# Router logits of a two-layer attention and expert kernel: each tile of 128 tokens in its own 32 columns of the array, one transpose for four tiles

## The chip, the core and the metric

The kernel runs on one core of a Trainium2 chip. A core has four engines that compute: TensorE (PE in the profile, with its weight loads as PEld), VectorE (DVE), ScalarE (ACT) and GpSimd (POOL); SyncE (SP) issues most transfers. Matmul results land in PSUM[...]; VectorE and ScalarE copy them on to SBUF. The metric is the time of one execution on the device, in microseconds; lower is better. Everything here is fp32.

## What is computed

The program is a stack of two layers over x of shape (4, 512, 256). Each layer is an attention over a context of 1024 rows, and then a mixture of experts with two experts for each token. The change concerns only the logits of the two routers:

```python
def _L0_ffn_ref(x, gate_w, expert_bias, w1, w2):
    logits = jnp.einsum('btd,ed->bte', x, gate_w) + expert_bias     # 8 experts and 4 "zero" ones
    topk_logits, topk_idx = jax.lax.top_k(logits, TOP_K)
    topk_w = jax.nn.softmax(topk_logits, axis=-1)
...
def _L1_ffn_ref(x, Wg, alpha, ln_w, ln_b, fc1_w, fc1_b, fc2_w, fc2_b):
    logits = xf @ Wg                                                # 8 experts
    top_vals, top_idx = jax.lax.top_k(logits, TOP_K)
    gate_score = jax.nn.softmax(top_vals, axis=-1)
...
x = x + _L0_xattn_ref(_layernorm(x, axis=-1), ctx_1024, ...)
x = x + _L0_ffn_ref(_layernorm(x, axis=-1), ...)
x = x + _L1_xattn_ref(_layernorm(x, axis=-1), ctx_1024, ...)
x = x + _L1_ffn_ref(_layernorm(x, axis=-1), ...)
```

## The kernel before

The work goes by batches of 512 tokens (four tiles of 128). `layer0_attention` runs the first attention batch by batch; `layer0_experts` computes keys and values for the second attention beside the last routing steps (`mha_kvs`), and then the expert tiles (`moe`, with `tile_turn`, `tile_up`, `tile_down`); `layer1_attention` runs 32 units of the second attention (a batch, a tile of tokens, a pair of heads each), with the routing of layer 1 and some expert tiles worked in; `layer1_experts` is the last stage, the rest of the second layer's expert tiles.

TensorE's instructions stand in the order in which the Python code issues them (`manual_schedule`); SyncE's too, in the expert stages. The other engines are ordered by a scheduler. What a change moves on those engines is read from the built program.

Routing is a generator, `route_steps(L, b)`, one for each layer and batch, whose steps are taken between pieces of other work. Its steps, each up to a `yield`:

1. `route_norm`: layer norm of x (L807 to L845).
2. Eight transposes of the normed rows into `xT`, [128 features, 2 halves, 512 tokens] (L237, copied out at L243, L245 and L247).
3. The logits, transposed (L858 to L865): two accumulating matmuls, with the router's weights (128 x 12 or 128 x 8) as the loaded operand and the 512 tokens as the moving one. The result, 12 or 8 partitions by 512 tokens, is copied to SBUF at L863 (layer 0, with the bias added for each partition) or at L865 (layer 1).
4. Four transposes, one for each tile of tokens, back to [128 tokens, tile, expert] (L869), a copy to `rt_lg` (L871), and `top2` (L745 to L777).
5. The counts of tokens for each expert and their running sums: two matmuls into `pos` (L886, L887), then each token's row in the experts' buffer, and the scatters to it on GpSimd's queue (L920).

When the last batch of a layer has been routed, `tile_table` makes the table of expert tiles. The first rows of the expert stage (L1182) are loaded after all scatters of the layer; their transposes (L1091) wait for them on TensorE.

PSUM pools of two buffers each: scores `ps_s`, transposes `ps_t`, and the rest `ps_m` (`mm_ps`), from which the logits, their transposes and the sums take a buffer, as do the queries (L586), keys (L485) and values (L499) around them.

Other places that are named below: `sim_finish` with the attended context (`hq`, L334), its product with the encoder (`ehT`, L338), the batch's summary (`hc`, L353 and L355; `hcc`, L382), the mixed weights (`weff`, L388) and the sums that use them (`hcq`, L370, added to x at L396); `sim_scores` (L304); `mha_scores` (L602, L611, L615), `mha_turn` (L625, L628, L630), and `mha_values` (L650), which computes two heads at once, each in its own 64 columns of the array:

```python
for j in range(NJ):
    for r in range(2):
        nc.tensor.matmul(
            op[r * HD : r * HD + HD, :], st["v"][:, j, bass.ts(2 * n + r, HD)], aT[:, r, bass.ts(j, P)],
            start=(j == 0), stop=(j == NJ - 1),
        )
```

The router's weights and bias are loaded once, on SyncE's queue behind the first loads of x and the context (L185 to L187).

Of the kernel before, what the change touches and what calls it, by code (L numbers as in the profile page):

```python
# [8 lines left out]
F32 = mybir.dt.float32  # L9
# [4 lines left out]
ALU = mybir.AluOpType  # L14
# [3 lines left out]
P = 128  # L18
NB = 4
S = 512  # L20
NT = S // P
# [3 lines left out]
NC = D // P  # L25
NH = 4
HD = 64
EX = 8
ET0 = 12
FF0 = 512  # L30
FF1 = 1024
# [2 lines left out]
REGION = NB * S  # L34
ROW = D + 2
TILES = NB * S * 2 // P + EX - 1
RING = 3
W1ROW = NC * FF1 + 2 * NC + FF1 // P
ATT_SCALE = 0.125
# [23 lines left out]
def two_layers(ctx: ExitStack, tc: tile.TileContext, io, out):  # L63
    nc = tc.nc

    const = ctx.enter_context(tc.tile_pool(name="const", bufs=1))
# [14 lines left out]
    def t4(shape, name, dt=F32):  # L81
        return k4.tile(shape, dt, tag="k4", name=name)
# [4 lines left out]
    def tsmall(shape, tag, dt=F32):  # L87
        return sm.tile(shape, dt, tag=tag, name=tag, bufs=2 if tag[:3] in ("rt_", "tp_", "tt_") else None)
# [7 lines left out]
    def mm_ps(name):  # L96
        return ps_m.tile([P, 512], F32, tag="m", name=name)


    ident = const.tile([P, P], F32, tag="ident", name="ident")  # L100
# [23 lines left out]
    nc.gpsimd.tensor_copy(base, base_i)  # L124
    tile_i = const.tile([P, TILES], I32, tag="tile_i", name="tile_i")
    nc.gpsimd.iota(tile_i, [[1, TILES]], base=0, channel_multiplier=0)
    tile_f = const.tile([P, TILES], F32, tag="tile_f", name="tile_f")
    nc.gpsimd.tensor_copy(tile_f, tile_i)
# [14 lines left out]
    def small(name, shape, src, queue=nc.sync):  # L143
        t = const.tile(shape, F32, tag=name, name=name)
        queue.dma_start(out=t, in_=src)
        return t
# [35 lines left out]
    for b in range(2, NB):  # L182
        load_x(b)
        last_load = load_ctxT(b)
    gate_w = small("gate_w", [P, NC, ET0], io["gate_wT"].rearrange("(c p) e -> p c e", p=P))  # L185
    gate_b = small("gate_b", [ET0, 1], io["expert_bias"])
    wg = small("wg", [P, NC, EX], io["Wg"].rearrange("(c p) e -> p c e", p=P))  # L187
    alpha = small("alpha", [P, EX], io["alpha"].partition_broadcast(P))
    fc2b = small("fc2b", [EX, D], io["fc2_b"])
    wq = small("wq", [P, NC, D], io["Wq"].rearrange("(c p) n -> p c n", p=P))  # L190
# [4 lines left out]
    for e in range(EX):  # L195
        i = nc.gpsimd.dma_start(
            out=rows[e * REGION : (e + 1) * REGION, :].rearrange("(p k) r -> p k r", p=P),
            in_=zeros.unsqueeze(1).to_broadcast([P, REGION // P, ROW]),
# [5 lines left out]
        out=ys[:, :].rearrange("(p k) d -> p k d", p=P),  # L204
        in_=zeros[:, 0:D].unsqueeze(1).to_broadcast([P, 2 * NB * S // P, D]),
# [34 lines left out]
    def to_sbuf(dst, src, name, only=None):  # L240
        for c, pt in transposed(src, name):
            if only is not None:
                L1.turned = only(dst[:, c, :], pt)  # L243
            elif c % 2 == 0:
# [155 lines left out]
    def layer0_attention():  # L400
# [31 lines left out]
        for b in range(NB):  # L432
# [32 lines left out]
            if more:  # L465
                turns(b + 1, 3)
            route = route_steps(L0, b)
            next(route)
        return route
# [198 lines left out]
    def layer1_attention(sts):  # L668
# [10 lines left out]
        for i in range(len(units) + 4):  # L679
# [44 lines left out]
            if k == 0 and 0 <= b < NB:  # L724
                routes[b] = route_steps(L1, b)
                next(routes[b])
        scatter_pending(2, L1.normed)
        for n in PIECES:
            for _ in range(n):
                next(tiles, None)  # L730
            for route in routes.values():
                next(route, None)
            if len(L1.run) < NB:
                scatter_pending(2, L1.turned)
            if len(L1.run) == NB and L1.table is None:
                L1.table = tile_table(L1)
# [40 lines left out]
        return w  # L777

    class Layer:
        def __init__(self, n, ne, nf, w, bias):  # L780
            self.n, self.ne, self.nf, self.w, self.bias = n, ne, nf, w, bias
            self.run = []
            self.state = {}
            self.done = None
            self.table = None

            self.first = (0, 0, 0) if n == 0 else (0, 0, 1)
            self.spread = []
            self.held = const.tile([P, RING], F32, tag=f"held{n}", name=f"held{n}")
            for s, e in enumerate(self.first):  # L790
                nc.gpsimd.memset(self.held[:, s : s + 1], float(e))

    L0 = Layer(0, ET0, FF0 // P, gate_w, gate_b)
    L1 = Layer(1, EX, FF1 // P, wg, None)
    scatters, row_loads, y_stores = [], [], []
    pending = []

# [49 lines left out]
    def route_steps(L, b):  # L847

        ne = L.ne
# [5 lines left out]
        only = nc.vector.tensor_copy if L.n == 1 and b + 1 == NB else None  # L855
        xT = to_sbuf(t4([P, NC, S], f"xn{L.n}rT_{b}"), L.state[b]["xn"], f"xn{L.n}rTp_{b}", only)
        yield
        lt_ps = mm_ps(f"lgT{L.n}_{b}")[0:ne, :]  # L858
        for c in range(NC):
            nc.tensor.matmul(lt_ps, L.w[:, c, :], xT[:, c, :], start=(c == 0), stop=(c == NC - 1))  # L860
        lt = t4([ET0, S], f"lgTs{L.n}_{b}")[0:ne, :]
        if L.bias is not None:
            nc.vector.tensor_scalar(lt, lt_ps, L.bias, None, ALU.add)  # L863
        else:
            nc.vector.tensor_copy(lt, lt_ps)  # L865
        yield
        lgp = mm_ps(f"lg{L.n}_{b}")[:, 0 : NT * ne].rearrange("p (t e) -> p t e", e=ne)
        for t in range(NT):
            nc.tensor.transpose(lgp[:, t, :], lt[:, bass.ts(t, P)], ident[0:ne, 0:ne])  # L869
        lg = tsmall([P, NT, ne], "rt_lg")  # L870
        nc.vector.tensor_copy(lg, lgp)  # L871
        st = L.state.pop(b)
        buf, xn = st["buf"], st["xn"]
        shape = [P, 2, NT, ne]
# [1 line left out]
        w = top2(lg, ne, pick)  # L876
# [16 lines left out]
        at = tsmall([P, NT, ne], "rt_atp")  # L893
# [81 lines left out]
    def tile_table(L):  # L975

        lim = L.run[NB - 1][:, 0:EX]
        big_shape = [P, TILES, EX]
        n = tsmall([P, EX], "tt_n")
# [18 lines left out]
        )  # L998
        ef = const.tile([P, TILES], F32, tag="tt_ef", name=f"tt_ef{L.n}")
        nc.vector.tensor_reduce(ef, past, AX.X, ALU.add)  # L1000
# [7 lines left out]
        nc.vector.tensor_tensor(tmp, past, step.unsqueeze(1).to_broadcast(big_shape), ALU.mult)  # L1008
        off = const.tile([P, TILES], F32, tag="tt_off", name=f"tt_off{L.n}")
        nc.vector.tensor_reduce(off, tmp, AX.X, ALU.add)  # L1010
# [5 lines left out]
        nc.vector.tensor_scalar(tab[:, 1, :], off, float(EX * REGION - P), None, ALU.min)  # L1016
        nc.vector.tensor_tensor(tab[:, 2, 0:RING], ef[:, 0:RING], L.held, ALU.not_equal)
        L.tabled = nc.vector.tensor_tensor(tab[:, 2, RING:], ef[:, RING:], ef[:, 0 : TILES - RING], ALU.not_equal)

# [22 lines left out]
    def ring_slots(L, slots=None):  # L1042
# [3 lines left out]
        if L.n == 0:  # L1046
            for s in range(RING):
                if s % 2 == 0:
# [3 lines left out]
        else:  # L1052
            slots = [loaded[s] if s in loaded else slot1(s) for s in range(RING)]
        for s in range(RING):
            if s not in loaded:
# [22 lines left out]
    def tile_turn(T, i, name, valid, aside, behind=None):  # L1078
# [13 lines left out]
        if n == 0:  # L1092
            L0.turned = nc.vector.tensor_copy(hT.rearrange("p c n -> p (c n)"), pt[:, 0:D])  # L1093
        else:
# [226 lines left out]
    def layer0_experts(route):  # L1321

        slots = ring_slots(L0)
        mask = mha_mask(0)

        def biases():
            for t in range(NT):
                after(mha_bias(sts[0], t), L0.turned, "a transfer does not hold up the tiles")
                yield
# [9 lines left out]
        sts[0]["mask"] = mask  # L1339
        moe(L0, slots, biases())  # L1340
        for _ in mha_kvs(sts, (2,)):
# [35 lines left out]
def _layouts(i):  # L1377

    import numpy as np

    def a(name):
        return np.asarray(i[name])

    def cols(v):
        v = v.reshape(*v.shape[:-1], v.shape[-1] // P, P)
        return np.moveaxis(v, -1, 0)

    def chunks(v):
        e, r, n = v.shape
        return v.reshape(e, r // P, P, n).transpose(0, 2, 1, 3).reshape(e, P, r // P * n)  # L1390

    ctx = a("ctx_1024")
    return {
        "x": a("x"),
        "ctx": ctx,
        "ctxT": ctx.transpose(0, 2, 1),
        "mask": a("mask_BxSxS2_bf1").view(np.uint8),
        "w_sim": cols(a("L0_xattn_w_sim").reshape(3, D)),
        "b_sim": a("L0_xattn_b_sim"),
        "W_qv": a("L0_xattn_W_qv"),  # L1400
        "b_qv": a("L0_xattn_b_qv"),
        "w_sim_row": a("L0_xattn_w_sim")[0:D],
        "gate_wT": a("L0_ffn_gate_w").T,
        "expert_bias": a("L0_ffn_expert_bias").reshape(ET0, 1),
        "w1p0": chunks(a("L0_ffn_w1").transpose(0, 2, 1)),
        "w2p0": chunks(a("L0_ffn_w2").transpose(0, 2, 1)),
        "Wq": a("L1_xattn_Wq"),
        "Wkv": a("L1_xattn_Wkv"),
        "Wo": a("L1_xattn_Wo"),
        "Wg": a("L1_ffn_Wg"),  # L1410
        "alpha": a("L1_ffn_alpha"),
        "w1p1": np.concatenate(
            [
                chunks(a("L1_ffn_fc1_w")),
                chunks(a("L1_ffn_ln_w")[:, :, None]),
                chunks(a("L1_ffn_ln_b")[:, :, None]),
                chunks(a("L1_ffn_fc1_b")[:, :, None]),
            ],
            axis=2,
        ),  # L1420
        "w2p1": chunks(a("L1_ffn_fc2_w")),
        "fc2_b": a("L1_ffn_fc2_b"),
    }
# [18 lines left out]
```

## Time and profile before

| what | us |
|---|---|
| median of three runs (lowest, highest) | 950.67 (949.68, 955.41) |
| the profiled execution | 946.2 |
| its span, from the first to the last instruction | 944.4 |
| TensorE busy in it | 888.6 |
| VectorE, ScalarE, GpSimd busy | 428.8, 331.2, 226.0 |
| logits' matmuls, L860, 32 records, busy | 15.0 |
| their transposes, L869, 32 records, busy | 3.3 |
| copies of the logits on VectorE, L863 and L865, 8 in all, busy | 5.7 |

Busy time in a profile is the union of an engine's records; where records of a pipelined engine overlap, the mean of one times their number is more than the busy time. The profile shows each fp32 matmul as two records and each transpose as one. A group of instructions is given by line, engine, operation, tiles (out<-in, with partitions x columns of the array), and its count; then busy us and mean ns of one, and the idle time of the engine just before it with what ended it. The granted clock of TensorE was 0.989 of full speed over this execution.

### The profile page before, as it was taken

Reading aid. Unit: us, or ns where it says so; the run is one execution under the profiler, and the core shown is the slowest. Engines: PE = TensorE matmul, PEld = TensorE weight load, DVE = VectorE, ACT = ScalarE, POOL = GpSimd, SP = SyncE. Lnnn points to the kernel's source line nnn. Section 1 sums busy time; section 2 is a strip of 40 time slices with the busy share of each in tenths; the row PEclk is TensorE's granted clock in tenths of the full one; section 3 lists DMA queues with packets and bytes.
Section 4 is the critical chain, followed back from the end, with each engine's and each line's share of the span. In section 5 each row is a group of like instructions: output and inputs, shape, how many; then the busy total and the mean of one; then the engine's idle time right before and its main releaser. Section 6 shows DMA issues by size and latency. Waiting matters only on the chain. (4 is left out here: it accounts for less than half of the span.)

```text
span 944.4 us, 15177 instructions
## 1 busy us (share of the span) xinstructions
PE 888.6 (94%) x5506; PEld 666.1 (71%) x5506; DVE 428.8 (45%) x1253; ACT 331.2 (35%) x734; POOL 226.0 (24%) x275
## 2 busy tenths in 40 slices
PE   5899999999999998999999999999989999999995
PEld 2455464645688997556675665667869999999995
DVE  5446473645623322775665776666631212121210
ACT  3322232221221111475664664565422322232221
POOL 2312014043412222000130250250741112211121
PEclk9899999999999999999999999999989999999999
DMA  9999912020178794600000122221236957777971
GB/s 311 292 254 245 285 57 86 37 98 27 54 259 260 225 324 148 223 23 1 24 1 1 46 71 110 68 69 46 74 90 215 325 152 250 213 251 231 320 236 16
DMA packets 54906, 142.05 MB, mean 150 GB/s; under 512 B 6774, under 2 KB 32813, under 8 KB 48680
## 3 DMA queue, kind: packets, MB, share of 16 engines
q1 hardware_dynamic: 39144, 102.89, 32.8%
q0 software_dynamic: 15392, 38.10, 15.6%
q8 instruction: 47, 0.77, 0.3%
q14 instruction: 35, 0.29, 0.1%
q10 hardware_dynamic: 288, 0.00, 0.0%
HBM read 131.51 MB, written 39.91 MB: 182 GB/s over the span
## 5 line engine op out<-in xcount | busy, mean ns | idle before, releaser
L1125 ACT ACTIVATE aT<-hp,w1s 128x128 f32<-128x128 f32 x248 | 67.3, 382 | 167.5 <-issue 153.2
L1116 PEld LDWEIGHTS hp<-hT,w1s 128*128 128x128 f32 x992 | 115.8, 192 | 2.3 <-DVE hT L1097 0.7
L1116 PE MATMUL hp<-hT,w1s 128*128 128x128 f32 x992 | 116.1, 275 | 0.5 <-DVE hT L1097 0.5
L1141 PE MATMUL y<-w2s,aT 128*128 128x256 f32 x496 | 112.3, 379 | 0.5 <-ACT aT L1125 0.5
L1141 PEld LDWEIGHTS y<-w2s,aT 128*128 128x128 f32 x496 | 91.8, 190 | 11.9 <-ACT aT L1125 0.7
L615 ACT ACTIVATE p<-p,s_nm 128x1024 f32<-128x1024 f32 x64 | 73.4, 1147 | 67.9 <-DVE s_nm L611 62.6
L611 DVE CUSTOM_DVE_ANT_0 p<-s,mbias 128x1024 f32<-128x1024 f32 x64 | 75.7, 1220 | 45.9 <-PE s L602 45.8
L1158 POOL DMA_INDIRECT out<-yw,to x31 | 47.8, 1541 | 178.3 <-DVE to L1082 102.8
L1145 DVE TENSOR_SCALAR yw<-y,row 128x256 f32<-128x256 f32 x59 | 28.5, 484 | 127.6 <-PE y L1141 127.6
L625 PEld LDWEIGHTS a2t<-ident,p 128*128 128x128 f32 x512 | 55.9, 141 | 41.6 <-issue 21.3
L920 POOL DMA_INDIRECT rows<-rowbuf,rt_posi x64 | 64.4, 1006 | 82.7 <-DVE rt_posi L900 26.6
L625 PE MATMUL a2t<-ident,p 128*128 128x128 f32 x512 | 71.5, 279 | 8.8 <-ACT a2T L630 4.2
L602 PE MATMUL s<-kT,q2T 64*128 64x512 f32 x256 | 66.6, 628 | 0.7 <-DVE s_nm L611 0.7
L650 PE MATMUL o<-a2T,v 128*64 128x128 f32 x1024 | 63.3, 276 | 0.1
L304 PE MATMUL s<-ctxT,q0T 128*128 128x512 f32 x128 | 61.7, 628 | 0.7 <-ACT q0T L281 0.7
L650 PEld LDWEIGHTS o<-a2T,v 128*64 128x64 f32 x1024 | 55.4, 137 | 8.5 <-issue 7.0
L630 ACT COPY a2T<-a2t 128x512 f32<-128x512 f32 x96 | 53.4, 581 | 20.9 <-PE a2t L625 20.6
L1097 DVE TENSOR_SCALAR hT<-ht,w1s 128x128 f32<-128x128 f32 x62 | 22.6, 405 | 81.8 <-PE ht L1091 79.9
L334 PE MATMUL hq<-a0T,ctxn 128*128 128x512 f32 x128 | 56.8, 596 | 0.1
L1116 PEld LDWEIGHTS hp<-hT,w0s 128*128 128x128 f32 x448 | 54.4, 192 | 2.9 <-DVE hT L1093 1.5
L1116 PE MATMUL hp<-hT,w0s 128*128 128x128 f32 x448 | 54.9, 275 | 1.0 <-DVE hT L1093 1.0
L1141 PE MATMUL y<-w0s,aT 128*128 128x256 f32 x224 | 53.1, 380 | 0.7 <-ACT aT L1121 0.7
(260 smaller groups left out, 1226.4 us busy)
## 6 DMA issues: line engine op xcount, KB each, us to landing
w1s<-in_w1p SPq DMA_DIRECT2D x34, 1030.0 KB
w2s<-in_w2p SPq DMA_DIRECT2D x34, 1024.0 KB
rows<-zeros POOLq DMA_DIRECT2D x8, 2064.0 KB
w0s<-in_w1p SPq DMA_DIRECT2D x31, 512.0 KB
w0s<-in_w2p SPq DMA_DIRECT2D x31, 512.0 KB
row<-rows SPq DMA_DIRECT2D x59, 129.0 KB
ctxT<-in_ctxT SPq DMA_DIRECT2D x4, 1024.0 KB
ctxn<-in_ctx SPq DMA_DIRECT2D x4, 1024.0 KB
```

What stands on the lines that cost most here:

```text
L304: nc.tensor.matmul(sp[:, h, :], st["qT"][:, c, bass.ts(t, P)], ctxT[b][:, c, bass.ts(h, 512)], start=(c == 0), stop=(c == NC - 1),)
L334: nc.tensor.matmul(op, ctxn[b][:, j, bass.ts(c, P)], aT[:, j, :], start=(j == 0), stop=(j == NJ - 1))
L602: nc.tensor.matmul(sps[r][:, k, :], st["qT"][at, n, bass.ts(t, P)], st["kT"][at, n, bass.ts(k, 512)], start=True, stop=True,)
L611: nc.vector.tensor_tensor_reduce(p, sps[r].rearrange("p h n -> p (h n)"), st["mbias"][:, t, :], -ATT_SCALE, -ATT_SCALE * LEAST, ALU.add, A ...
L615: nc.scalar.activation(p, p, AF.Exp, bias=nm, scale=-1.0, accum_out=tot[:, r : r + 1])
L625: nc.tensor.transpose(pt[:, bass.ts(j, P)], p[:, bass.ts(4 * g + j, P)], ident)
L630: nc.scalar.copy(d, pt)
L650: nc.tensor.matmul(op[r * HD : r * HD + HD, :], st["v"][:, j, bass.ts(2 * n + r, HD)], aT[:, r, bass.ts(j, P)], start=(j == 0), stop=(j == ...
L920: i = nc.gpsimd.indirect_dma_start(out=rows[:, :], out_offset=bass.IndirectOffsetOnAxis(ap=pos_i[:, k, t : t + 1], axis=0), in_=buf[:, k, ...
L1116: nc.tensor.matmul(o, w1[:, c * ff + f * P : c * ff + f * P + P], hT[:, c, :], start=(c == 0), stop=(c == NC - 1),)
L1125: nc.scalar.activation(aT[:, f, :], hp[:, f // 4, bass.ts(f % 4, P)], AF.Gelu_apprx_tanh, bias=w1[:, at : at + 1])
L1141: nc.tensor.matmul(op, aT[:, f, :], w2[:, f * D : f * D + D], start=(f == 0), stop=(f == nf - 1))
```

## The change

The weights of both routers come into one tile, `gates`, 32 columns wide for each half of the features: layer 0's 12 columns, then layer 1's 8, and zeros. Either layer multiplies by all 32 columns. Each of the four tiles of tokens is a matmul of its own, 128 tokens wide, whose result lies in its own 32 partitions of PSUM. So one 128 x 128 copy and one 128 x 128 transpose serve all four tiles; the layer's columns are picked in reading the transposed result. Layer 0's bias is no longer added for each partition in the first copy but from a row that is spread over all partitions, in the second. The matmuls go by half and then by tile, so that consecutive matmuls go to different groups of columns.

```diff
+GROUP = 32
...
-    gate_w = small("gate_w", [P, NC, ET0], io["gate_wT"].rearrange("(c p) e -> p c e", p=P))
-    gate_b = small("gate_b", [ET0, 1], io["expert_bias"])
-    wg = small("wg", [P, NC, EX], io["Wg"].rearrange("(c p) e -> p c e", p=P))
+    gates = const.tile([P, NC, GROUP], F32, tag="gates", name="gates")
+    nc.gpsimd.memset(gates, 0.0)
+    for src, at, n in ((io["gate_wT"], 0, ET0), (io["Wg"], ET0, EX)):
+        nc.sync.dma_start(out=gates[:, :, at : at + n], in_=src.rearrange("(c p) e -> p c e", p=P))
+    gate_b = small("gate_b", [P, ET0], io["expert_bias"].partition_broadcast(P))
...
-    L0 = Layer(0, ET0, FF0 // P, gate_w, gate_b)
-    L1 = Layer(1, EX, FF1 // P, wg, None)
+    L0 = Layer(0, ET0, FF0 // P, 0, gate_b)
+    L1 = Layer(1, EX, FF1 // P, ET0, None)
...
-        lt_ps = mm_ps(f"lgT{L.n}_{b}")[0:ne, :]
+        lt_ps = mm_ps(f"lgT{L.n}_{b}")[:, 0:P]
         for c in range(NC):
-            nc.tensor.matmul(lt_ps, L.w[:, c, :], xT[:, c, :], start=(c == 0), stop=(c == NC - 1))
-        lt = t4([ET0, S], f"lgTs{L.n}_{b}")[0:ne, :]
+            for t in range(NT):
+                nc.tensor.matmul(
+                    lt_ps[t * GROUP : t * GROUP + GROUP, :], gates[:, c, :], xT[:, c, bass.ts(t, P)],
+                    start=(c == 0), stop=(c == NC - 1),
+                )
+        lt = t4([P, P], f"lgTs{L.n}_{b}")
+        nc.vector.tensor_copy(lt, lt_ps)
+        yield
+        lgp = mm_ps(f"lg{L.n}_{b}")[:, 0:P]
+        nc.tensor.transpose(lgp, lt, ident)
+        lgp = lgp.rearrange("p (t e) -> p t e", e=GROUP)[:, :, L.at : L.at + ne]
+        lg = tsmall([P, NT, ne], "rt_lg")
         if L.bias is not None:
-            nc.vector.tensor_scalar(lt, lt_ps, L.bias, None, ALU.add)
+            nc.vector.tensor_tensor(lg, lgp, L.bias.unsqueeze(1).to_broadcast([P, NT, ne]), ALU.add)
         else:
-            nc.vector.tensor_copy(lt, lt_ps)
-        yield
-        lgp = mm_ps(f"lg{L.n}_{b}")[:, 0 : NT * ne].rearrange("p (t e) -> p t e", e=ne)
-        for t in range(NT):
-            nc.tensor.transpose(lgp[:, t, :], lt[:, bass.ts(t, P)], ident[0:ne, 0:ne])
-        lg = tsmall([P, NT, ne], "rt_lg")
-        nc.vector.tensor_copy(lg, lgp)
+            nc.vector.tensor_copy(lg, lgp)
```

In the built program TensorE and ScalarE have their instructions at the same places as before, but for the logits and their transposes themselves. GpSimd has one more, the memset of `gates`, behind the issue of `wsim_row`; the first load into `gates` waits for it. SyncE issues the bias after both weights instead of between them. On VectorE the logits' copy stands ahead of `ehT` (L338) in layer 0's first three batches, where it stood behind it, and in layer 1's second batch ahead of a piece of the mask (L525).

More of the change, by code (lines that the diff above doesn't have):

```diff
@@ L779, in two_layers, with __init__ @@
     class Layer:
-        def __init__(self, n, ne, nf, w, bias):
-            self.n, self.ne, self.nf, self.w, self.bias = n, ne, nf, w, bias
+        def __init__(self, n, ne, nf, at, bias):
+            self.n, self.ne, self.nf, self.at, self.bias = n, ne, nf, at, bias
             self.run = []
@@ L1403, in _layouts @@
         "gate_wT": a("L0_ffn_gate_w").T,
-        "expert_bias": a("L0_ffn_expert_bias").reshape(ET0, 1),
+        "expert_bias": a("L0_ffn_expert_bias"),
         "w1p0": chunks(a("L0_ffn_w1").transpose(0, 2, 1)),
```

## The prediction

> **What bounds the kernel now.** I read the page first (busy time, then the slices), then the waits of TensorE, then the groups by shape for the lines that the change touches, and last the timeline at those lines, because only there does one see when the next instruction starts.
>
> ```profile
> span 944.4 us, 15177 instructions
> PE 888.6 (94%) x5506; PEld 666.1 (71%) x5506; DVE 428.8 (45%) x1253; ACT 331.2 (35%) x734; POOL 226.0 (24%) x275
> ...
> PE   5899999999999998999999999999989999999995
> ```
> ```profile
> PE eTp L237 <- DVE xn L226: 7.6, 1, 7.6
> PE ht L1091 <- DMA row<-rows: 6.2, 4, 3.9
> PE a0t L263 <- ACT q0T L281: 4.7, 3, 2.4
> PE a2t L625 <- ACT a2T L630: 4.2, 6, 1.8
> ```
>
> TensorE (PE) is busy 94% of the span and in nearly every slice. The waits (total us, times, longest) are single ones of a few microseconds: the start (7.6), the rows at the heads of the expert stages (6.2), some steps of the attentions. So time taken off PE's stream is worth its own length, unless the next wait on another engine swallows it. The page's chain of what ended last covers only 0.2% of the span and carries nothing here.
>
> The routers' logits are computed eight times: batches 0 to 3 of layer 0 from 108.3 to 233 us, of layer 1 from 505.2 to 673 us. By shape (busy us, mean ns, idle before):
>
> ```profile
> L650 PE MATMUL o<-a2T,v 128*64 128x128 f32 x1024 | 63.3, 276 | 0.1
> L860 PE MATMUL lgT<-xn0rT,gate_w 128*12 128x512 f32 x16 | 7.5, 594 | 0.0
> L860 PE MATMUL lgT<-xn1rT,wg 128*8 128x512 f32 x16 | 7.5, 593 | 0.0
> L863 DVE TENSOR_SCALAR lgTs<-lgT,gate_b 12x512 f32<-12x512 f32 x4 | 3.0, 738 | 4.7 <-PE lgT L860 4.7
> L865 DVE COPY lgTs<-lgT 8x512 f32<-8x512 f32 x4 | 2.7, 676 | 4.4 <-PE lgT L860 4.4
> L860 PEld LDWEIGHTS lgT<-xn0rT,gate_w 128*12 128x12 f32 x16 | 1.2, 92 | 5.7 <-issue 5.7
> ```
>
> Two matmuls of a batch appear as four records: each fp32 matmul is two passes. Now the timeline (start, length) of the first batch's logits and its transposes:
>
> ```profile
> 107.73 0.59 PE L334 MATMUL hq<-a0T,ctxn 128*128 128x512 f32 x1
> 108.26 1.89 PE L860 MATMUL lgT<-xn0rT,gate_w 128*12 128x512 f32 x4
> 110.07 1.12 PE L304 MATMUL s<-ctxT,q0T 128*128 128x512 f32 x2
> ```
> ```profile
> 126.09 0.38 PE L370 MATMUL hcq<-weff,eT 128*128 128x256 f32 x1
> 126.40 0.41 PE L869 MATMUL lg<-ident,lgTs 12*128 12x12 f32 x4
> 126.74 0.44 PE L263 MATMUL a0t<-ident,p 128*128 128x128 f32 x2
> ```
>
> Single records start at 108.26, 108.69, 109.12 and 109.55: 0.43 us for 512 columns, 0.107 for 128. Going into the narrow matmuls costs 0.10 (0.53 instead of 0.43 from 107.73 to 108.26), leaving them 0.09 (0.52 from 109.55 to 110.07). The transposes hold PE from 126.30 (126.09 plus 0.21 for 256 columns) to 126.74: 0.44.
>
> **The nearest row for the new form** is the values of attention, L650: it too alternates between groups of columns (two of 64), with 128 moving columns.
>
> ```profile
> 413.77 1.97 PE L650 MATMUL o<-a2T,v 128*64 128x128 f32 x32
> 415.67 0.33 PE L656 MATMUL o<-ident,s_rs 128*128 128x128 f32 x1
> ```
> ```profile
> 414.04 0.14 PEld L650 LDWEIGHTS o<-a2T,v 128*64 128x64 f32 x2
> ```
> ```profile
> 414.15 0.14 PEld L650 LDWEIGHTS o<-a2T,v 128*64 128x64 f32 x2
> ```
>
> 32 records take 1.90 us to the next start, 59 ns each, where 128 columns alone take 107. The last two fences are the loads seen at two moments 0.1 us apart: they come in pairs, a pair every 0.107. I read it so: the second pass of a matmul must wait until the first has streamed through the same group, and the first pass of the next matmul, in another group, starts right beside it. Then the price is one 128-column stream per matmul of two passes, whether there are two groups or four.
>
> **The change part by part.**
>
> *Logits.* 8 matmuls of 128 columns (16 records) in place of 2 of 512 (4 records). Streaming before: 4 x 0.427 = 1.71. After, at the pace of L650: 8 x 0.107 = 0.86. The 0.10 before and 0.09 behind stay, since the old matmuls were narrow too. Gain 0.85 a batch, 6.8 in all. Bounds: four groups wholly at once give 4 x 0.107 = 0.43 (gain 1.28, 10.2 in all); no overlap gives 16 x 0.107 = 1.71 (gain 0). I take L650, the same engine, dtype and moving width.
>
> *A rule against and one for.* The Trainium skill ("TensorE: Matmul & The Clock Gate", Part 3, The mechanism) says that a weight load overlaps matmuls in flight only if it goes to other row groups. All four new groups span all 128 rows, so by that rule each record would pay its load too: 16 x (0.092 + 0.107) = 3.18, a loss of 1.47 a batch. L650 spans all rows as well and runs at 59 ns a record, not at 0.137 (its load) + 0.107, so the row decides. The skill's "TensorEngine Tiling (Array Packing)" (Theoretical Speedup) gives up to 4x for a dimension of at most 32: 0.43 us. L650 has groups enough for its 2x and reaches 107/59 = 1.8, but the pairs above are no sign that four groups would do better; I keep 0.86.
>
> *Transposes.* One of 128x128 in place of four of 12 (or 8) rows: 0.107 of stream, no change of array form, instead of 0.44: gain 0.33 where PE goes on to something ready. That is four places (layer 0 batches 0 and 1, layer 1 batches 2 and 3). In layer 1, batches 0 and 1, the next matmul (q, L586) waits for the PSUM buffer that L871 frees; from 515.82 to 516.51 now, some 0.15 less then. In layer 0 the third is followed by a wait for DVE's x (0.17), the fourth by v, which waits until DVE has copied k (236.15 to 236.84): 0.1 and 0. Sum 4 x 0.33 + 2 x 0.15 + 0.1 = 1.7.
>
> *VectorE.* The copy out of PSUM goes from 512 to 128 elements a partition: 738 or 676 ns become about 290 (L659, 128x128 from PSUM, took 287). 3.3 us less on DVE, but nothing on the path: the transposes that need it start at 126.4, fifteen us after it, and even in the two tight places (copy ends 234.98 and 674.74) PE comes 1 us later. L871 becomes an add with a broadcast bias in layer 0: 128x48 with a broadcast is 208 ns at L760, a copy 193. The built order puts the copy ahead of ehT (L338) in layer 0. DVE then stands until the logits end, near 109.3, so ehT ends about 110.3 instead of 109.67; who waits are the hcq matmuls, behind s (from 110.07, 3.3 us) and hc. For batch 2 there is no s: hcq starts at 211, logits end near 208.5, ehT near 209.6. Cover 1 us.
>
> *Loads.* SP issues three transfers as before, two into one tile. The first now waits for POOL's memset of that tile, which comes after the DMA issue at 4.04 and ahead of the memsets at 4.66; SP reaches it at 17.57. Behind it stand alpha, fc2b, wq, wkv, wo and ctxn; 12 us of cover, cost 0. The bias row grows to 6 KB over 128 partitions, like alpha (0.46 to issue), first used at 126.9. The memset takes about 0.2 (a 128x128 one did) while POOL idles until 11.45: 0.
>
> *What is late next.* At the heads of the expert stages PE waits for rows whose addresses come from the last batch's logits. At 703.65 (3.9 us) the chain back runs over scatters, table, pos at 680.05 and lg at 676.15, which stood in PE's order behind lgT at 672.13, not at a DMA. So the wait keeps its length and moves forward.
>
> Sum: 6.8 + 1.7 = 8.5 off PE. Waits on ACT and DVE in the attentions (a2t on a2T 4.2, on xn2T 2.7) will swallow some; I take off 1.5. Forecast -7.0: the profiled execution, 946.2 us with a span of 944.4, becomes 939.2. That execution is 0.5% below the median of the runs, 950.67; in its terms 950.67 x 939.2 / 946.2 = 943.6.
>
> **The rivals.**
>
> *All four groups at once.* For: the loads are short (92 ns for 12 columns), and four disjoint groups could stream together. Against: passes issue in order, and L650 shows a pair each 107 ns. Gain 10.2 + 1.7 - 1.5 = 10.4: 940.2.
>
> *No gain.* Groups of 32 don't overlap (no row of the trace has four), or the time stands before the next wait; the transposes alone give 1.7, less what is swallowed: -2 to +1, 949 to 952.
>
> *Slower: exposed weight loads.* Sixteen loads a batch instead of four, each before its stream, as the quoted rule has it. Per record 0.092 + 0.107 = 0.199; +1.47 a batch, +11.8 in all, less 1.7: +10.1, 960.8. It decides at 0.12 us a record ((1.71 + 0.21) / 16, where the transposes' gain per batch is counted): above that the change loses. For: the loads double in number per column streamed. Against: L650.
>
> **How the numbers follow.** What the measurement can tell from no change is about 1%, 9.5 us. Forecast 0.60 (a tenth of it, or scatter of the runs, falls beyond 1%); all at once 0.16, mostly beyond 1%; no gain 0.17; slower 0.07, its price just at the bound. Faster 0.22, same 0.72, slower 0.06. Likeliest 943.6. The range takes in all at once and no gain, with a scatter of 2 to 3 us (the three runs span 5.7): 937 to 953.
>
> **What would show it.** Right: L860 with 16 records a batch, the next PE start about 1.05 us after the first instead of 1.81; the next start after L869 within 0.15 instead of 0.34; the DVE copy near 0.29; PE busy down by 7 to 9; the wait at the second expert stage still near 3.9. Wrong: records of L860 0.107 or more apart (no gain, or slower beyond 0.12), about 0.03 apart (all at once), or PE's idle time grown by what its busy time lost (swallowed).

## The result, and the profile after

The changed kernel took 939.43 us (median of four runs, 936.1 to 940.3), the kernel before 950.17 beside it (four runs, 947.21 to 955.41): a ratio of 0.9873, with a 95% interval of 0.9838 to 0.9909. That is 1.3% faster, past the 1% that the prediction took as the limit of what can be told (the interval begins at 0.9%). The profiled execution took 939.67, with a span of 937.9.

In the changed kernel's code the logits are L867, their copy L872, the transposition L875, and the copy to `rt_lg` L879 (layer 0, an addition) or L881; the queries are L590, the values of attention L654, the values of the context L503.

The page: the span, and busy time by engine.

```profile
span 937.9 us, 15324 instructions
PE 875.9 (93%) x5578; PEld 663.0 (71%) x5578; DVE 426.8 (46%) x1253; ACT 331.5 (35%) x734; POOL 226.4 (24%) x276
```

TensorE's busy time fell by 12.7 us (888.6 to 875.9), the span by only 6.5: its idle time rose by 6.2. At the changed lines 10.7 of the busy time went (9.8 for the logits, 0.9 for the transpositions); of the rest, some 1.7 can be put down to the granted clock, which fell once less in this execution (four times, against five; the last section has what such a dip is). So more was taken off than predicted, and more was given back.

The groups by shape at the changed lines (busy us, mean ns of one, idle before):

```profile
L867 PE MATMUL lgT<-xn1rT,gates 128*32 128x128 f32 x64 | 2.6, 279 | 0.0
L867 PE MATMUL lgT<-xn0rT,gates 128*32 128x128 f32 x64 | 2.6, 279 | 0.0
L875 PE MATMUL lg<-ident,lgTs 128*128 128x128 f32 x8 | 2.4, 298 | 0.0
L872 DVE COPY lgTs<-lgT 128x128 f32<-128x128 f32 x8 | 2.3, 289 | 19.0 <-PE lgT L867 15.5 <-remote 3.5
```

The logits' busy time is 5.2 us in place of 15.0. The copy takes 289 ns, as forecast. Now the timeline of TensorE at the first batch's logits and at its transposition (start, length):

```profile
107.38 1.02 PE L338 MATMUL hq<-a0T,ctxn 128*128 128x512 f32 x2
108.34 0.64 PE L867 MATMUL lgT<-xn0rT,gates 128*32 128x128 f32 x16
108.91 1.98 PE L308 MATMUL s<-ctxT,q0T 128*128 128x512 f32 x4
...
124.28 1.03 PE L374 MATMUL hcq<-weff,eT 128*128 128x256 f32 x4
125.23 0.33 PE L875 MATMUL lg<-ident,lgTs 128*128 128x128 f32 x1
125.40 1.04 PE L267 MATMUL a0t<-ident,p 128*128 128x128 f32 x8
```

Sixteen records, and the next matmul starts 0.57 us after the first of them, where it was 1.81 before and 1.05 was predicted. Behind the transposition it starts after 0.17, where it was 0.34.

Where this went is read from the starts of TensorE's instructions in both profiled executions (us):

| stretch | before | after | gain |
|---|---|---|---|
| from a batch's logits to its transposition, 8 stretches: 18.14, 18.14, 10.54, 3.73, 10.59, 10.56, 8.80, 4.02 before | 84.52 | 75.51 | 9.01 |
| of these, layer 1, batch 1 | 10.56 | 10.29 | 0.27 |
| from the transposition of layer 0, batch 3, to the values of the context (L499, L503) | 0.86 | 1.81 | -0.95 |
| first expert stage, from its first `hp` to the keys behind it | 112.53 | 114.73 | -2.20 |
| from the last transposition to the last group of `y` (L1141, L1151) | 255.45 | 256.10 | -0.65 |

Seven of the eight stretches gained 1.06 to 1.35, about what the logits themselves did (1.24). One gained almost nothing. The waits of TensorE name what came in (total us, times, longest):

```profile
PE ht L1101 <- DMA row<-rows: 7.8, 4, 4.1
...
PE a2t L629 <- ACT a2T L634: 4.2, 6, 1.8
PE a2t L629 <- DVE xn2T L584: 2.7, 5, 1.1
...
PE v L503 <- DVE kT L496: 1.5, 1, 1.5
...
PE q L590 <- DVE oT L663: 1.0, 1, 1.0
```

The two waits that the prediction named as swallowers, of `a2t` on `a2T` and on `xn2T`, stand at 4.2 and 2.7 as before. New among these is the wait of `q` for `oT`. The timeline of all engines at that place, layer 1, batch 1:

```profile
570.23 1.15 ACT L619 ACTIVATE p<-p,s_nm 128x1024 f32<-128x1024 f32 x1
...
570.37 0.64 PE L867 MATMUL lgT<-xn1rT,gates 128*32 128x128 f32 x16
...
571.37 0.25 ACT L662 COPY s_rT<-o 128x128 f32<-128x128 f32 x1
...
571.66 0.29 DVE L663 TENSOR_TENSOR oT<-o,s_rT 128x128 f32<-128x128 f32 x1
...
572.00 1.98 PE L590 MATMUL q<-xn2T,wq 128*128 128x512 f32 x4 [0.99 <-DVE oT L663]
```

ScalarE is in an exponential when the logits start, so it copies `s_rT` at 571.37 and VectorE computes `oT` at 571.66, whatever TensorE does. Before, 1.8 us of logits covered that; 0.57 do not. Nothing in `q` needs `oT`: it multiplies x by weights. What it can need is the PSUM buffer that `oT` is read from.

### The profile page after: what moved, and what is told of

It is laid out like the page before. It is cut to its first block, busy times and chain, and to the rows that moved or that the text cites. A ratio compares the mean times of both kernels' runs of the same rounds, so it can differ in the third digit from the quotient of the medians.

```text
span 937.9 us, 15324 instructions
## 1 busy us (share of the span) xinstructions
PE 875.9 (93%) x5578; PEld 663.0 (71%) x5578; DVE 426.8 (46%) x1253; ACT 331.5 (35%) x734; POOL 226.4 (24%) x276
## 5 line engine op out<-in xcount | busy, mean ns | idle before, releaser
L1151 PE MATMUL y<-w2s,aT 128*128 128x256 f32 x496 | 112.3, 379 | 0.5 <-ACT aT L1135 0.5
L1151 PEld LDWEIGHTS y<-w2s,aT 128*128 128x128 f32 x496 | 91.8, 190 | 11.9 <-ACT aT L1135 0.7
L654 PE MATMUL o<-a2T,v 128*64 128x128 f32 x1024 | 63.3, 276 | 0.1
L654 PEld LDWEIGHTS o<-a2T,v 128*64 128x64 f32 x1024 | 55.4, 137 | 8.5 <-issue 6.8
L338 PE MATMUL hq<-a0T,ctxn 128*128 128x512 f32 x128 | 56.8, 596 | 0.1
L1151 PE MATMUL y<-w0s,aT 128*128 128x256 f32 x224 | 53.1, 380 | 0.7 <-ACT aT L1131 0.7
```

The lines of the kernel that those rows point to most:

```text
L338: nc.tensor.matmul(op, ctxn[b][:, j, bass.ts(c, P)], aT[:, j, :], start=(j == 0), stop=(j == NJ - 1))
L654: nc.tensor.matmul(op[r * HD : r * HD + HD, :], st["v"][:, j, bass.ts(2 * n + r, HD)], aT[:, r, bass.ts(j, P)], start=(j == 0), stop=(j == ...
L1151: nc.tensor.matmul(op, aT[:, f, :], w2[:, f * D : f * D + D], start=(f == 0), stop=(f == nf - 1))
```

## The experiments

All were timed beside the kernel before, whose medians were 950.34, 950.55, 949.96 and 949.69, in the four groups of runs that follow.

**The change again.**

> The change as it is, against the kernel before, for a tighter ratio and a second profile. If the gain is what the two profiled spans say (944.4 to 937.9, 6.5 us), the ratio lies near 0.993; if it is what the first timed runs say (0.9873), near 0.987. In the profile, either way: 16 records of the logits within 0.64 us, TensorE busy near 876, and one batch's gain from one logits' start to the next step near 1.25 us. If the 1.5 us wait of v (L503) in layer 0's last batch belongs to the change, it is there again; if it was a stall of that one execution (the copy of the logits started 1.3 us after they were ready), it is about 0.5.

937.71 us, ratio 0.9862 (0.9838 to 0.9886), and a span of 934.4. So the gain is 1.3 to 1.4%, some 12 us, and the first pair of profiles shows too little of it. The first expert stage took 110.14 us here, against 112.53 before and 114.73 in the first execution after: the 2.2 us lost there were chance, in the waits for rows (4.3 us in all, all of it at the second expert stage, against 7.8). The wait of `q` for `oT` was there again, 1.0.

**The order of the passes.** Tile after tile, both halves of a tile in succession, so that consecutive matmuls go to the same group of columns:

```diff
-        for c in range(NC):
-            for t in range(NT):
+        for t in range(NT):
+            for c in range(NC):
```

> The same 8 matmuls, ordered by tile and then by half, so that the four passes of one group of columns follow each other. If each group of columns streams its own passes from a queue of its own (groups independent of the order), the logits still take 0.43 us of streaming and the time is that of the change. If passes start strictly in the order of the program, each waiting for the one before in its group (as the prediction read L650), a batch takes 12 x 0.107 + 0.107 = 1.39 us, 0.96 more than the change, 7.7 us in all: near the kernel before.

938.48 us, ratio 0.9867 (0.9843 to 0.9892): as the change. The timeline at the first logits:

```profile
109.15 0.67 PE L867 MATMUL lgT<-xn0rT,gates 128*32 128x128 f32 x16
109.74 0.70 PE L308 MATMUL s<-ctxT,q0T 128*128 128x512 f32 x1
```

0.59 us to the next start. If passes started strictly in the order in which they are written, a tile's four passes would each wait for the one before, and the four tiles could overlap only at their ends. They overlap nearly whole: the single records start in fours, 13 ns apart, and a four every 0.11 us (109.15, 109.28, 109.39, 109.50). So a matmul that waits for its own group does not hold back one for another group; that was the prediction's argument against the full overlap.

**Two groups instead of four.** The same sixteen records with the same 32-column loads, but only two groups, each used for two tiles in turn (and two transpositions of 64 rows):

```diff
-        lt_ps = mm_ps(f"lgT{L.n}_{b}")[:, 0:P]
+        lt_ps = mm_ps(f"lgT{L.n}_{b}")[0 : 2 * GROUP, 0 : 2 * P]
...
+        for h in range(2):
+            for c in range(NC):
+                for g in range(2):
...
+                        lt_ps[g * GROUP : g * GROUP + GROUP, bass.ts(h, P)], gates[:, c, :],
+                        xT[:, c, bass.ts(2 * h + g, P)], start=(c == 0), stop=(c == NC - 1),
```

> The same 16 records with loads of 32 columns, but in two groups of columns (tiles 0 and 2 in the first, 1 and 3 in the second), and two transposes of 64 rows. If the pace is set by the streams of 128 columns in each group (0.107 each, 8 a group), the logits take 0.86 us of streaming, 0.43 more than the change: 3.4 us more in all, and records start in pairs each 0.107. If it is set by the loads[...], they take 0.43 as in the change.

941.64 us, ratio 0.9907 (0.988 to 0.9933), 3.9 us above the change beside it.

```profile
109.07 1.07 PE L868 MATMUL lgT<-xn0rT,gates 128*32 128x128 f32 x16
110.07 0.70 PE L308 MATMUL s<-ctxT,q0T 128*128 128x512 f32 x1
```

1.00 us to the next start instead of 0.57: what counts is how many streams a group carries one after another (eight of 0.107, against four), not how many loads are issued.

**The same pieces in one group.** The kernel before, each half cut into four matmuls of 128 columns:

```diff
-        for c in range(NC):
-            nc.tensor.matmul(lt_ps, L.w[:, c, :], xT[:, c, :], start=(c == 0), stop=(c == NC - 1))
+        for t in range(NT):
+            for c in range(NC):
+                nc.tensor.matmul(
+                    lt_ps[:, bass.ts(t, P)], L.w[:, c, :], xT[:, c, bass.ts(t, P)], start=(c == 0), stop=(c == NC - 1)
+                )
```

> The kernel before with each half's matmul of 512 tokens cut into four of 128, all in one group of columns, transposes as before. If the gain comes from groups side by side, the 16 records stream one after another, 16 x 0.107 = 1.71 us, and the time is that of the kernel before (within 2 us). If it comes from shorter matmuls, it is that of the change; if 12 more loads (0.09 each) stand in the stream, 1.1 us a batch is lost, 9 us in all.

950.02 us, ratio 0.9996 (0.9975 to 1.0016).

```profile
107.31 1.92 PE L861 MATMUL lgT<-xn0rT,gate_w 128*12 128x128 f32 x16
109.16 0.70 PE L304 MATMUL s<-ctxT,q0T 128*128 128x512 f32 x1
```

1.85 us. Sixteen loads for four cost 0.03 us a batch (1.848 for 1.817); the cut by itself gains nothing. With one, two and four groups, sixteen records of 128 columns take 1.85, 1.00 and 0.57 us (in one group with loads of 12 or 8 columns, otherwise of 32).

**Other PSUM buffers.** Can the new waits be had back? First only the turned logits from the transposes' buffers (the last pair of lines), then both, beside the change once more:

```diff
-        lt_ps = mm_ps(f"lgT{L.n}_{b}")[:, 0:P]
+        lt_ps = tr_ps(f"lgT{L.n}_{b}")[:, 0:P]
...
-        lgp = mm_ps(f"lg{L.n}_{b}")[:, 0:P]
+        lgp = tr_ps(f"lg{L.n}_{b}")[:, 0:P]
```

> The change again, run beside the two kernels with other buffers. Expected ratio to before 0.987 (between 0.984 and 0.990), as in the two measurements there are. In its profile PE should again wait 1.0 us for oT ahead of q in layer 1, 0.3 us twice for the buffer that the copy of lg frees, and about 0.95 us for the copied k ahead of v. If the waits for oT and for kT do not come back, they were chance of an execution and not a price of the change.

> The change, with the turned logits (lg) taken from the PSUM buffers of the transposes instead of those of the matmuls. My theory: what the change gains beyond its own records is partly given back in waits that were covered before. The waits of q for the copy of lg (0.3 us twice) should go and the wait of v for kT (0.95) may get shorter: 0.6 to 1.5 us less than the change beside it, ratio to before about 0.986. Rival (these waits are swallowed by the next wait on ACT or DVE anyway): the same time as the change, within 0.3 us. A second rival: the buffers of the transposes come free later, so that the transposes of the attentions wait in their place: 1 us or more slower than the change.

> As the one before, and the logits themselves (lgT) from the buffers of the transposes too. If q in layer 1 waits for oT because the logits take a buffer of the matmuls that q then has to wait for, the 1.0 us goes too: 1.5 to 2.5 us less than the change, ratio about 0.985. If q waits for the data in oT (the chain from the exponentials over the sums to oT, which 1.8 us of logits covered before and 0.57 us do not), the 1.0 us stays, and the time is that of the kernel before it in this list. The rival of later buffers would show as waits of the transposes (a2t, xn1rTp) longer than in the change, and a time above it.

935.55 us, ratio 0.9844 (0.9811 to 0.9877), for the change; 936.95, 0.986 (0.9826 to 0.9894), for the first; 936.66, 0.9849 (0.9821 to 0.9877), for the second: not to be told apart. Waits of TensorE in the change:

```profile
PE q L590 <- DVE oT L663: 1.0, 1, 1.0
...
PE v L503 <- DVE kT L496: 0.7, 1, 0.7
PE q L590 <- DVE rt_lg L881: 0.6, 2, 0.3
```

and in the second of the two:

```profile
PE a2t L629 <- DVE lgTs L872: 0.6, 1, 0.6
...
PE a0t L267 <- DVE rt_lg L879: 0.3, 2, 0.2
```

In the second the wait for `oT` is gone, in the first it stayed at 1.0. So it was a wait for a buffer. But the transposes' buffers are wanted too: `a2t` and `a0t` wait there now. In both kernels the stretch from layer 0's last transposition to the first expert tile took 26.1 us, against 24.95 in the change. Waits do not explain that: the one of the routing sums for `rt_wk` was 1.4 instead of 0.8, but the one for `kT` had gone. The granted clock does. In both, the second half of the values took 5.41 us instead of 3.69:

```profile
235.77 5.41 PE L503 MATMUL v<-wkv,ctxT 128*128 128x256 f32 x16 [0.45 <-ACT v L511]
```

The clock stood at 0.50 there for 3.4 us, which is 1.7 us lost; without them the stretch is 24.4, shorter than the change's. Whether the other waits brought that dip is not shown.

**The buffers where they pay.**

```diff
-        lt_ps = mm_ps(f"lgT{L.n}_{b}")[:, 0:P]
+        lt_ps = (tr_ps if (L.n, b) == (1, 1) else mm_ps)(f"lgT{L.n}_{b}")[:, 0:P]
...
-        lgp = mm_ps(f"lg{L.n}_{b}")[:, 0:P]
+        lgp = (tr_ps if L.n else mm_ps)(f"lg{L.n}_{b}")[:, 0:P]
```

> The change, with buffers of the transposes only where they took a wait away and brought none: the logits of layer 1, batch 1 (ahead of q, which waited 1.0 us for the buffer that oT frees) and the turned logits of layer 1 (q waited 0.3 us twice for the copy of lg). If these waits are a matter of buffers, all three go, no new wait of a0t or a2t comes (0.17 twice and 0.59 in the kernel before this one), and the execution is 1.6 us shorter than the change at the same granted clock: ratio to before about 0.985. If later waits swallow what is taken away, the waits for oT and rt_lg go and others on ACT or DVE grow by as much: ratio as the change, 0.987. The two ratios lie within what the timing can tell apart; the profile's waits and the starts at the stages' marks decide.

935.6 us, ratio 0.9849 (0.9811 to 0.9887). None of the three waits is in its profile, and none of `a2t` or `a0t` for the logits. From batch 1's logits to `q`, and from its transposition to the next `q`:

```profile
566.13 0.64 PE L867 MATMUL lgT<-xn1rT,gates 128*32 128x128 f32 x16
566.71 1.55 PE L590 MATMUL q<-xn2T,wq 128*128 128x512 f32 x3
...
575.37 0.27 PE L875 MATMUL lg<-ident,lgTs 128*128 128x128 f32 x1
575.48 1.88 PE L590 MATMUL q<-xn2T,wq 128*128 128x512 f32 x4
```

0.58 us instead of 1.63, and 0.11 instead of 0.61 (twice): 2.05 us in all. Yet its span is 934.1, that of the change beside the earlier two 934.2. The granted clock tells why: in its profile seven stretches of 3.4 us run at half the clock, in the other four. One of them, seen in a window of 1 us (busy us of each engine, then the granted clock), and the scores in it:

```profile
616.00:617.00 1.00, 1.00 (x4) 0.34 (x2) 0.00 (x0) 0.00 (x0) 0.69 (x2) 0.50 0.79 278
```

```profile
615.31 3.66 PE L606 MATMUL s<-kT,q2T 64*128 64x512 f32 x8
618.90 1.10 PE L629 MATMUL a2t<-ident,p 128*128 128x128 f32 x8
```

The same eight records in the change:

```profile
617.57 1.99 PE L606 MATMUL s<-kT,q2T 64*128 64x512 f32 x8
619.49 1.09 PE L629 MATMUL a2t<-ident,p 128*128 128x128 f32 x8
```

3.59 us to the next start against 1.92: 1.67 us went.

So both were measured once more, on one chip:

> The change, for a comparison with the kernel beside it on the same chip. Over all runs so far a thousandth of the granted clock is worth about 0.8 us, and at the same granted clock the change lies 11.4 us below before. Expected: ratio 0.985 to 0.988, and the runs on that line (938 at 0.987, 936.5 at 0.989). In the profile q waits again 1.0 us for oT and twice 0.3 for rt_lg.

> The kernel with the other buffers where they pay, beside the change this time. If the three waits that it removes are its gain, it lies 1.6 us below the change at the same granted clock (the runs so far gave 3.1, on another chip, with an uncertainty of 1.7). Rival: later waits swallow it, and it lies within 0.5 us of the change. In its profile the stretch from the first logits of layer 1 to the addition before the second expert stage (180.1 us in the change at full granted clock) should take 178.5, plus what a dip of the granted clock adds.

939.11 us, ratio 0.9898 (0.9867 to 0.993), for the change, a smaller gain than the 0.985 to 0.988 that was expected; 938.82, 0.9892 (0.9857 to 0.9927), for the other: by the medians the same. By the stretch that was named: the other took 180.8 us, of which the clock's dips (three times 3.4 us at half the clock) cost 5.1, which leaves 175.7; its first run, treated so, has 176.2. The 180.1 that the expectation called free of dips hold one of 1.7; without dips the four profiles of the change have 178.4 to 179.3. So in this stretch, at full clock, the other kernel is shorter by 2.2 us or more.

The time does not show it. One straight line of time against granted clock for each kernel, with one slope for all, fitted afterwards over all runs of this study but two of the kernel before at 961 us, puts the other 2.2 us below the change at the same clock (standard error 0.7; twelve and twenty-two runs). But its clock was lower, 0.9852 in the mean against 0.9876, and the mean times are both 937.9. If fewer waits bring more dips, a comparison at the same clock leaves out their price. Whether they do, or both are chance, no run here decides; so no gain of time is shown for the other buffers.

## Why the prediction was right, and where only the sum was

The total was right: 943.6 predicted, 939.43 measured, inside the range. The direction was right; the share between faster and the same was not, since 72 in 100 were given to within 1%. By the medians the forecast gain of 7 us was 10.7, and the first rival, all four groups at once, had said 940.2, which is nearer.

*Logits: mis-sized, and for a wrong reason.* The term was 0.85 us a batch, on the reading that passes issue in order and a second pass holds up the rest. Measured: 1.24, and for all eight, with the waits that came in right behind them, 8.5 instead of 6.8. The lower bound of the working (0.43 of stream, four groups wholly at once), which made the first rival, is what the runs show: the order hardly matters (0.59 tile by tile), the number of groups does (1.85, 1.00, 0.57). L650's 59 ns a record was the pace of two groups, not of any number; its pairs every 0.107 become fours every 0.11. The row was read rightly as a measurement and wrongly as a mechanism, and the estimate was carried from two groups to four by the mechanism.

*The rule against.* The Trainium skill ("TensorE: Matmul & The Clock Gate", Part 3, The mechanism) would have loads overlap only with other row groups, a loss of 1.47 a batch; no run shows such a cost. (The same section also lets a load go ahead that is meant for the background weight buffer; the prediction left this out.) The up to 4x of "TensorEngine Tiling (Array Packing)" (Theoretical Speedup) is met but for the changes of form at the ends: 1.81 to 0.57 to the next start, with 0.10 into the narrow matmuls as before (107.38 to 108.34 is two starts of 512 columns at 0.43, and 0.10).

*Transposes: mis-sized by a quarter.* In layer 1, batches 2 and 3, the term of 0.33 was right: from the matmul ahead to the one behind it was 0.60 and 0.54 before (647.52 to 648.12, 675.95 to 676.49) and 0.27 and 0.22 in the repeat beside the buffers' kernels. In layer 0, batches 0 and 1, only 0.19 came: the 0.10 ahead of the transposition stayed (124.28 and four matmuls of 0.21 make 125.13; it starts at 125.23), where the prediction had put it down to the narrow form. It is a wait for a buffer, which VectorE's addition to x sets free:

```profile
125.23 0.14 PEld L875 LDWEIGHTS lg<-ident,lgTs 128*128 128x128 f32 x1 [0.32 <-DVE x L400]
```

With the transposes' buffers the same place takes 0.33 (125.43 to 125.76) instead of 0.47, and the whole 0.33 of the prediction is there. Where `q` waits for the buffer it was 0.08 and 0.18 in place of 0.15 each, and where PE waits for x or for the keys nothing. That makes 1.3 for 1.7.

*Swallowed: mis-sized, and in other places.* 1.5 us was taken off for `a2t`, which lost nothing. In the first execution after, 1.0 went to the buffer that `oT` frees, 0.95 to the copied keys, 2.2 to the rows of the first expert stage, 0.65 behind the last transposition. The first is a price of the change: it came back in every repeat of it. The keys' wait, 1.5 in the first execution, was 0.9, 0.7 and 1.5 in the repeats; at 0.7 the values start 0.95 after the transposition, hardly later than the 0.86 of before. The rows' was chance. So, it seems, was the 0.65: the same stretch took 256.7 and 255.4 in the first two repeats. The prediction looked at the longest waits of before and asked which would grow; the one that came was hidden under the very instructions that were cut short.

*Why the total came out.* In the first pair of profiles the larger gain and the larger loss made -6.5 for -7.0 forecast, by chance. The medians moved by 10.7. The difference lies in that one execution before: with a granted clock of 0.989 it is at the low end of its kernel's runs (946.2; of the 53 beside the experiments all but those two lie between 944.97 and 957.78). At the same granted clock the line above puts the change 10.9 us below before (standard error 0.5). The profiles locate some 9 of these: from the first logits of layer 0 to its last transposition 127.8 us became 122.4, the same in all four profiles of the change; the stretch of layer 1 named above, without dips, went from 182.8 to between 178.4 and 179.3; and up to 0.95 went to the keys. Where the rest lies is open.

*The rest held.* The copies on VectorE (0.29), the loads and the memset cost nothing that shows, `ehT` behind the logits' copy had its cover, and the wait at the second expert stage kept its length (3.95 before, 4.12 after) and moved. "Exposed weight loads" and "no gain" are refuted by the runs with one, two and four groups: twelve more loads in one group cost 0.03 us a batch.

## What to carry to other kernels

Narrow matmuls of independent tiles (here 12 or 8 columns, filled up to 32) can each have their own group of columns: the stream then took a quarter, in both orders of issue that were tried, and one transposition did for four. Read a row of the trace as a pace for its own shape, and before carrying it to another shape ask which mechanism would scale it; here one run with two groups would have told. Where an instruction on the critical engine gets shorter, look at what ran on the other engines in its shadow, and at which PSUM buffer the next instruction takes: that wait is not in the profile of before. And when a wait is taken away, look at the time itself: here the waits went, and the mean time stayed.

## What the runs showed of the hardware that was not expected

Much of the scatter of this kernel's times comes from dips of the granted clock. In a dip it stands at 0.50 for 3.4 us and 1.7 us of TensorE's work go; some dips follow each other at once. The twelve profiled executions had between four and eleven, the fall at the very end left out, often at the same stages (near 35 and 555 us, and around the start of the second expert stage). Some come after TensorE has waited for some 2 us, others while it is busy: in the change beside the first two of the other buffers, one began at 680.4, with TensorE idle for only 0.15 of the 6.8 us ahead of it. A thousandth of the mean granted clock went with 0.9 us of time (standard error 0.07), which is a thousandth of the span. What sets off a dip, and whether the change itself draws fewer (mean granted clock 0.9876 over its runs, 0.9863 over those of before), was not tried.

Why VectorE's copy of layer 0's last logits started within 0.1 us of their end in some executions and 0.9 to 1.6 after it in others, while GpSimd issued its scatters one behind another, stays open; it moves the copied keys and so the 0.7 to 1.5 us above.
